# One PSUM bank for a sort opened earlier, and a block's transposes halved, in a graph-network kernel

## The chip, the core and the metric

The kernel runs on one core of a Trainium2 chip. A core has five engines, each with its own in-order list of instructions: TensorE (PE in the profile; its weight loads are PEld), VectorE (DVE), ScalarE (ACT), GpSimd (POOL) and SyncE (SP). They work side by side and wait for one another through semaphores. SP, ACT and POOL also issue DMAs. Matmuls write into PSUM, which has eight banks of 2 KB per partition; the other working memory is SBUF. The metric is the device time of one execution in microseconds.

## The reference

The input is a batch of 16 graphs: `x` (16, 1024, 64), a symmetric 0/1 adjacency `adj` (16, 1024, 1024) with a unit diagonal, and a node mask. Four graph layers follow one another, each in the form

```python
h = jnp.maximum(_layernorm(x, axis=-1), 0.0)
x = x + layer(h, adj, ...)
```

Layer 0 thins out the neighbours of nodes with many of them, and then takes, for each node and channel, three quantiles (0.25, 0.5, 0.75) over the values of the remaining neighbours, weights them by 0.25, 0.5, 0.25 into `agg`, and applies a two-layer perceptron to `h + agg`. Its core is

```python
vals = jnp.where(nd[..., None], x[:, None, :, :], jnp.inf)
s = jnp.sort(vals, axis=2)
v_lo = jnp.take_along_axis(s, idx_lo, axis=2)[:, :, 0, :]
v_hi = jnp.take_along_axis(s, idx_hi, axis=2)[:, :, 0, :]
agg = agg + w * (v_lo + frac * (v_hi - v_lo))
```

Layer 1 is a gated recurrent update of a message `A @ m`. Layer 2 is a message `adjacency @ h` and a small perceptron. Layer 3 is an attention over the adjacency with a softmax and `attention @ h`.

## The kernel before

The 16 graphs are worked on as 8 pairs (numbered 0 to 7 here). For a pair, these pieces of work exist:

- **The sort** (`sort_begin`, `sort_pair`). The 64 channels of two graphs fill 128 partitions, and a bitonic network of 55 steps sorts 1024 nodes in each. `sort_begin` loads x (L700), normalizes it (lines L662 to L672, with a Sqrt on ACT in L666), writes h_d and p_d, and transposes h on PE into a PSUM tile `ps` (L714), which ACT copies out (L717). A step of the network is three DVE operations: which pairs swap (L729), the larger (L736), the smaller (L737). Four steps' masks go to DRAM in one DMA (m_d, L740). Then the network is run backwards on the ranks with the masks read again (`swapped`, L749; DVE lines L753, L754, L760): the way back. At the end the ranks are transposed on PE into `ps` (L799), copied by ACT (L800) and written (y_d, L802). Tables of value differences go to t_d and w_d.
- **Neighbours** (`neighbours`, called by `prepare`). The adjacency is loaded in 512 KB blocks (`a`, L819, two buffers), thinned out with scans on DVE (L820, L825), squares on ACT (L854 to L856) and block matmuls on PE (L875), and a transposed copy is written to DRAM (a_d, L834).
- **The selection** (`weights`, `select`), once for each graph of the pair. Counting matmuls (L1045) and their evictions find each node's place in the sorted list; transposes (L1101) and sign evictions (L1103) make step functions of them; matmuls with tables of differences (L1148) and predicated copies (L1156) give the values. A compact step (from L1207) gathers up to 64 nodes of each graph that fall outside the windows of the first pass.
- **The extra block** (`extras`), once for a pair. The gathered rows are loaded (`comb_x`, L1257). In each of three rounds, ACT shifts them into `y_x` (L1275, two buffers), PE transposes 16 chunks of 128 x 112 into the PSUM tile `tr` (L1282), ACT makes two sign tiles of it (L1285), and DVE takes maxima of `y_x` in place (L1289, L954, L950, L1295, L1296). Some 25 small DVE operations (`places`) follow. Then six sums: PE fills `cand` (L1306, one buffer of four banks), DVE picks (L1011) and adds (L1018, L1020). Last, a selection matrix `sel_t` (one buffer, loaded on SP, L1314) puts the results back: a matmul into `tr` (L1317) and a predicated copy (L1318), once per graph.
- **The layers** (`layers`), for the pair's two graphs with separate pools: the perceptron and layers 1 to 3. The adjacency's transposed blocks are loaded three times (adjT, L1402) and multiplied (L1409). The last operations of a graph's DVE work are L1516 and L1519 of the attention.

The loop over pairs writes: selection of pair `pr`, the extra block, the layers, then neighbours and sort of pair `pr + 1`, and then `sort_begin` of pair `pr + 2`. The order on the engines is not the written order. A scheduler at build time takes the instructions by priority, as soon as by its own estimate their inputs and buffers are ready, and lays them down as one fixed list per engine. So sort steps and neighbours of a later pair stand among the instructions of the selection and the layers. Buffers of one name rotate in the written order: the sort's rows, `code` and masks of pair `pr + 2` follow those of `pr + 1`, and `sort_begin` of `pr + 2` needs the tile `ps` after `sort_pair` of `pr + 1`.

PSUM sets one limit. In the second half of the loop's body, `nbp` (neighbours) has two banks. During the extra block, `xp` has `tr` (two banks) and `cand` (four): all eight are taken. During the layers, `lb0` has three banks, `lb1` two and the sort's pool `sop` one: eight again. `sop` is opened when `xp` is closed, so the sort's two transposes, the one that ends a sort (L799) and the one that begins the next (L714), come after the extra block.

Of the kernel before, what the change touches and what calls it, by code (L numbers as in the profile page):

```python
# [9 lines left out]
F32 = mybir.dt.float32  # L10
BF16 = mybir.dt.bfloat16
# [3 lines left out]
I16 = mybir.dt.int16  # L15
F16 = mybir.dt.float16
F8 = mybir.dt.float8e5
AF = mybir.ActivationFunctionType
ALU = mybir.AluOpType
AX = mybir.AxisListType  # L20
PSUM = bass.MemoryType.PSUM
DRAM = bass.MemoryType.DRAM

P = 128
# [11 lines left out]
NH = NW // 2  # L36
# [6 lines left out]
def gnn_stack(ctx, tc, x, adj, nodemask, w, out):  # L43
# [10 lines left out]
    nc = tc.nc  # L54
    B, N, C = x.shape
# [9 lines left out]
    ident_b = const.tile([P, P], BF16, name="ident_b")  # L65
# [876 lines left out]
    NQ = C // 4  # L942
    SHR, SHL, AND, XOR = ALU.logical_shift_right, ALU.logical_shift_left, ALU.bitwise_and, ALU.bitwise_xor

    def maxima(yu, n):

        while n > 1:
            if n % 2 and n > 3:
                n -= 1
                nc.vector.tensor_tensor(  # L950
                    yu[:, :, :, :4], yu[:, :, :, :4], yu[:, :, :, n * 4 : n * 4 + 4], op=ALU.max
                )
            h = n // 2
            nc.vector.tensor_tensor(  # L954
                yu[:, :, :, : h * 4], yu[:, :, :, : h * 4], yu[:, :, :, (n - h) * 4 : n * 4], op=ALU.max
            )
            n -= h
# [66 lines left out]
    before = (half, lower)  # L1024
# [226 lines left out]
    def extras(pr, kept, aggs, xs, xp):  # L1251

        vx = kept["vx"]
        comb = xs.tile([P, NW * C], F32, name="comb_x")
        for u in range(0, len(PIECES), 2):
            at = slice(PIECES[u] * 512, (PIECES[u] + len(PIECES[u : u + 2])) * 512)
            nc.scalar.dma_start(comb[:, at], x_d[:, at])  # L1257
        tabs = []
        for i in range(2):
            tab = xs.tile([4 * NH, NQ, 4, 48], F16, name=f"tab{i}")  # L1260
            nc.vector.memset(tab, 0.0)
            for d in range(4):
                taken = nc.sync.dma_start(
                    tab[d : 4 * NH : 4, :, d, :],
                    t_d[(pr * 2 + i) * C : (pr * 2 + i + 1) * C, :NH].rearrange("(q d) h e -> d h q e", d=4)[d],
                )
            tabs.append(tab)
        qx = xs.tile([P, 3], F32, name="qx")
        nc.vector.tensor_scalar(qx, vx[:, :3], -2048.0, -2048.0, op0=ALU.mult, op1=ALU.add)
        signs = []  # L1270
        z = xs.tile([P, 1, 6, C], U16, name="z_x")
        odd = xs.tile([P, 1, 6, C], U16, name="odd_x")
        for k in range(3):
            y = xs.tile([P, 2, 2 * NQ, 4 * NH], I16, name="y_x", bufs=2)
            nc.scalar.activation(  # L1275
                y[:, 0].rearrange("p r (h d) -> p r h d", d=4),
                comb.rearrange("p (h r d) -> p r h d", r=2 * NQ, d=4),
                AF.Identity, bias=qx[:, k : k + 1], scale=1.0,
            )
            pt = xp.tile([P, 2, 512], F32, name="tr").bitcast(BF16).rearrange("p e (q n) -> p (e q) n", n=P)  # L1280
            for q in range(NQ):
                nc.tensor.transpose(pt[: 4 * NH, q, :], y[:, 0, q, :].bitcast(BF16), ident_b)  # L1282
            for s in range(2):
                sign = xs.tile([4 * NH, NQ, P], F16, name="sign_x", bufs=6)
                nc.scalar.activation(  # L1285
                    sign, pt[: 4 * NH].bitcast(I16), AF.Sign, bias=before[s][: 4 * NH], scale=-1.0
                )
                signs.append(sign)
            nc.vector.tensor_scalar_add(y[:, 1], y[:, 0], 2048.0)  # L1289
            yu = y.bitcast(U16)  # L1290
            maxima(yu, NH)
            ev, od = yu[:, :, :NQ, :4], yu[:, :, NQ:, :4]
            zs = z[:, 0, 2 * k : 2 * k + 2, :].rearrange("p s (q d) -> p s q d", d=4)
            os_ = odd[:, 0, 2 * k : 2 * k + 2, :].rearrange("p s (q d) -> p s q d", d=4)
            nc.vector.tensor_tensor(zs, ev, od, op=ALU.max)  # L1295
            nc.vector.tensor_tensor(os_, od, ev, op=ALU.is_gt)  # L1296
        marks = places(xs, z, 6 * C, 1)
        aggx = xs.tile([P, C], F32, name="agg_x")
        ag = aggx.rearrange("p (q d) -> p q d", d=4)
        for s in range(6):  # L1300
            cand = xp.tile([P, NQ, P], F32, name="cand")
            for q in range(NQ):
                for part in range(2):
                    for i in range(2):
                        mine = slice(i * ROOM, (i + 1) * ROOM)
                        nc.tensor.matmul(  # L1306
                            cand[mine, q, :96], signs[s][:, q, mine], tabs[i][:, q, :, part * 24 : (part + 1) * 24],
                            start=(part == 0), stop=(part == 1),
                        )
            v = pick(cand[:, :, :96], [mk[:, 0, s, :] for mk in (odd, *marks)])  # L1310
            add_to(ag, s == 0, v, vx[:, 3 + s : 4 + s])
        for i in range(2):
            sel_t = xs.tile([P, NT, P], F32, name="sel_t")
            nc.sync.dma_start(sel_t, sel_d[i])  # L1314
            ps = xp.tile([P, 2, 512], F32, name="tr")[:, 0, :].rearrange("p (t c) -> p t c", c=C)
            for t in range(NT):
                nc.tensor.matmul(ps[:, t, :], sel_t[:, t, :], aggx, start=True, stop=True)  # L1317
            nc.vector.copy_predicated(  # L1318
                aggs[i], kept["flag"][i].rearrange("p (t o) -> p t o", o=1).to_broadcast([P, NT, C]), ps
            )  # L1320
        return taken.ins if hasattr(taken, "ins") else taken
# [230 lines left out]
    def side_pools():  # L1552
        return (
            tc.tile_pool(reuse_waits="tile", name="nb", bufs=1),
            tc.tile_pool(reuse_waits="tile", name="nbp", bufs=2, space=PSUM),
        )

    pairs = B // 2
    nb_, nbp_ = side_pools()
# [7 lines left out]
    for pr in range(pairs):  # L1567
        with tc.tile_pool(reuse_waits="tile", name="keep", bufs=1) as keep:
            aggs = [keep.tile([P, NT, C], F32, name=f"agg{i}") for i in range(2)]
            kept = {  # L1570
                "flag": [keep.tile([P, NT], U16, name=f"flag{i}") for i in range(2)],
                "vx": keep.tile([P, 9], F32, name="vx"),
            }
            with tc.tile_pool(reuse_waits="tile", name="kn", bufs=1) as kn:
                with (
                    tc.tile_pool(reuse_waits="tile", name="sy", bufs=2) as sy,
                    tc.tile_pool(reuse_waits="tile", name="sw", bufs=1) as sw,
                    tc.tile_pool(reuse_waits="tile", name="sg", bufs=2) as sg,
                    tc.tile_pool(reuse_waits="tile", name="sp", bufs=2, space=PSUM) as sp,
                    tc.tile_pool(reuse_waits="tile", name="sc", bufs=2, space=PSUM) as sc,  # L1580
                ):
                    for i in range(2):
                        wt, positive = weights(pr * 2 + i, kn, None if i else taken)
                        select(pr * 2 + i, i, wt, positive, *made[i], aggs[i], kept, sw, sg, sy, sc, sp)
            nb_, nbp_ = side_pools()
            with nb_ as nb, nbp_ as nbp:
                with tc.tile_pool(reuse_waits="tile", name="xs", bufs=1) as xs, tc.tile_pool(reuse_waits="tile", name="xp", bufs=1, space=PSUM) as xp:
                    taken = extras(pr, kept, aggs, xs, xp)
                with (
                    tc.tile_pool(reuse_waits="tile", name="ly0", bufs=1) as ly0,  # L1590
                    tc.tile_pool(reuse_waits="tile", name="ly1", bufs=1) as ly1,
                    tc.tile_pool(reuse_waits="tile", name="lb0", bufs=3, space=PSUM) as lb0,
                    tc.tile_pool(reuse_waits="tile", name="lb1", bufs=2, space=PSUM) as lb1,
                    tc.tile_pool(reuse_waits="tile", name="sop", bufs=1, space=PSUM) as sop,
                ):
                    for i, (ly, lb) in enumerate(((ly0, lb0), (ly1, lb1))):
                        layers(pr * 2 + i, (pr * 2 + i) % 4, aggs[i], ly, lb)
                    if pr + 1 < pairs:
                        made = prepare(pr + 1, nb, nbp)
                        sort_pair(pr + 1, cur, sop)  # L1600
                    if pr + 2 < pairs:
                        cur = sort_begin(pr + 2, sop)
# [47 lines left out]
```

## Time and profile before

| | us |
|---|---|
| median of 3 runs | 6483.81 |
| lowest and highest run | 6482.19, 6496.31 |
| span of the profiled execution | 6475.2 |
| DVE busy | 5339.2 (82%) |
| PE busy | 4545.8 (70%) |
| ACT busy | 3530.8 (55%) |
| one pair in the middle of the run, from attention's end to attention's end | 775 |

The profile is of one execution. Its busy times per engine are sums over the whole span; the slices cut the span in 40 equal parts and give the busy share in tenths. A row of busy times by stage gives the stretch's start and end, its length, and then for each engine the busy time and the number of instructions in it, the granted TensorE clock, the DMA share and the GB/s. A row of a group of instructions gives the line, engine, operation, tiles and shapes, the count, then busy time and mean ns of one, and last the idle time of that engine just before them with what ended it. The span is 6.99 us under the lowest run's time and 8.61 us under the median.

### The profile page before, as it was taken

What the parts mean: (1) busy time and instruction counts of PE and PEld (TensorE: products, weight loads), DVE (VectorE), ACT (ScalarE), POOL (GpSimd) and SP (SyncE); (2) the same over time, 40 slices, a digit from 0 to 9 for tenths busy, and PEclk for the clock granted to TensorE, in tenths of its full rate; (3) what the DMA queues carried; (4) which work ended last, traced back from release to release, by engine and by line L of the source; (5) the groups of instructions that cost most, each with busy time, mean ns of one, the idle gap of its engine ahead of it and who ended that gap; (6) DMA issues with size and microseconds to landing.
All of it is one profiled execution on the core that took longest, in us unless ns stands there. A gap on an engine that the chain in (4) does not pass through costs nothing.

```text
span 6475.2 us, 112886 instructions
## 1 busy us (share of the span) xinstructions
PE 4545.8 (70%) x45010; PEld 2849.6 (44%) x45010; DVE 5339.2 (82%) x13031; ACT 3530.8 (55%) x4337; POOL 138.4 (2%) x234
## 2 busy tenths in 40 slices
PE   3177766776777858678577776777766776778856
PEld 2144542544435544355433554345543544435542
DVE  7999979997699976999679986899869997576655
ACT  4165555655556555556555565565565655555623
POOL 1000000000000000000000000000000000000000
PEclk7588868888788978888788886888868887788967
DMA  4311254112531126211361104511154112520014
GB/s 121 98 38 47 73 157 146 44 54 71 170 114 46 46 74 205 71 54 34 99 207 55 55 23 135 188 49 50 53 150 148 42 52 67 174 75 16 7 57 140
DMA packets 525639, 568.14 MB, mean 88 GB/s; under 512 B 265004, under 2 KB 414894, under 8 KB 525102
## 3 DMA queue, kind: packets, MB, share of 16 engines
q1 hardware_dynamic: 381472, 476.43, 24.1%
q10 hardware_dynamic: 142862, 82.31, 4.1%
q8 instruction: 355, 5.82, 0.4%
q0 software_dynamic: 768, 2.10, 0.1%
q14 instruction: 182, 1.49, 0.1%
HBM read 376.95 MB, written 183.76 MB: 87 GB/s over the span
## 4 chain that ended last, share of the span: by engine, by line
PE 36%; DVE 33%; ACT 13%; DMA 10%; issue 7%; SPq 1%; POOL 0%; ACTq 0%; DVEq 0%; POOLq 0%
PE comb L1045 13%; PE cand L1148 6%; ACT sign L1103 5%; DMA adjT<-a_d 4%; DVE y L1119 4%; PE comb L1101 3%; PE bank L1409 3%; PE comb L1236 2%; DVE att L1519 2%; DVE cand L1156 2%; DVE cum L825 2%; DMA a<-in_adj_dram 2%; DVE code L760 2%; DVE adjT L1513 2%; ACT y L1055 2%
## 5 line engine op out<-in xcount | busy, mean ns | idle before, releaser
L1045 PE MATMUL comb<-wt,ndT 128*128 128x512 fp8e5 x6144 | 1503.0, 401 | 26.1 <-DVE top L1516 11.1
L1055 ACT ACTIVATE y<-comb,qb 128x1024 int16<-128x1024 f32 (+1 forms) x640 | 632.0, 1026 | 954.0 <-PE comb L1045 953.5
L1045 PEld LDWEIGHTS <-ndT 128*128 128x128 fp8e5 x6144 | 615.3, 103 | 794.4 <-issue 188.5
L1119 DVE TENSOR_TENSOR y<-y 128x512 uint16<-128x512 uint16 (+5 forms) x896 | 705.3, 790 | 92.6 <-PE comb L1101 60.0
L1148 PE MATMUL cand<-vtab,sign 128*128 128x48 f16 (+1 forms) x18432 | 701.9, 194 | 105.1 <-DVE agg L1018 53.7
L1148 PEld LDWEIGHTS <-sign 128*128 128x128 fp8e5 x18432 | 668.0, 98 | 174.9 <-issue 76.8
L1101 PE MATMUL comb<-ident_b,y 128*128 128x128 bf16 x4608 | 392.2, 254 | 413.1 <-ACT sign L1103 363.1
L1103 ACT ACTIVATE sign<-comb,half 128x2048 fp8e5<-128x2048 int16 (+1 forms) x384 | 591.9, 1541 | 140.0 <-PE comb L1101 130.7
L1156 DVE COPY_PREDICATED cand<-w_f,cand 128x256 f32<-128x256 uint16 (+1 forms) x1536 | 535.2, 378 | 137.4 <-PE cand L1148 134.0
L1103 ACT ACTIVATE sign<-comb,lower 128x2048 fp8e5<-128x2048 int16 (+1 forms) x384 | 591.3, 1540 | 0.0
L1101 PEld LDWEIGHTS <-y 128*128 128x128 bf16 x4608 | 357.4, 115 | 437.1 <-issue 430.5
L1409 PE MATMUL bank<-adjT,nd 128*64 128x512 f32 x1024 | 304.4, 657 | 66.4 <-DMA adjT<-a_d 65.5
L1409 PE MATMUL bank<-att,hs 128*64 128x512 f32 x512 | 195.6, 871 | 202.7 <-ACT hs L1524 200.9
L729 DVE TENSOR_TENSOR swapped<-s 128x512 uint16<-128x512 f32 x440 | 301.5, 685 | 41.6 <-ACT s L717 36.6
L825 DVE TENSOR_TENSOR_SCAN cum<-ni 128x1024 f16<-128x1024 fp8e5 x128 | 292.9, 2290 | 41.9 <-ACT sq L854 23.6
L875 PE MATMUL pk<-minus_b,rem 128*128 128x128 bf16 x1024 | 222.4, 245 | 132.2 <-ACT rem L856 132.2
L875 PE MATMUL pk<-ident_b,ni 128*128 128x128 bf16 x1024 | 219.4, 241 | 129.3 <-ACT ndT L881 68.4
L833 ACT COPY at<-pk 128x512 f32<-128x512 f32 x256 | 146.7, 587 | 289.5 <-PE pk L831 139.2
L736 DVE TENSOR_TENSOR s<-s 128x512 f32<-128x512 f32 (+2 forms) x440 | 288.9, 657 | 0.0
L921 DVE TENSOR_SCALAR wt<-node 128x2048 uint8<-128x2048 f16 x224 | 269.3, 1217 | 23.6 <-PE comb L1236 23.5
L737 DVE TENSOR_TENSOR s<-s 128x512 f32<-128x512 f32 (+2 forms) x440 | 288.7, 656 | 0.0
L760 DVE TENSOR_TENSOR code<-code,xo 128x1024 uint16<-128x1024 uint16 x360 | 264.8, 736 | 5.2
(301 smaller groups left out, 8100.0 us busy)
## 6 DMA issues: line engine op xcount, KB each, us to landing
adjT<-a_d SPq DMA_DIRECT2D x384, 512.0 KB
a<-in_adj_dram SPq DMA_DIRECT2D x128, 512.0 KB
a_d<-at ACTq DMA_DIRECT2D x256, 256.0 KB
m_d<-swapped SPq DMA_DIRECT2D x104, 512.0 KB
swapped<-m_d SPq DMA_DIRECT2D x104, 512.0 KB
n_d<-nat SPq DMA_DIRECT2D x128, 128.0 KB
x_d<-xr SPq DMA_DIRECT2D x48, 256.0 KB
comb_x<-x_d ACTq DMA_DIRECT2D x24, 512.0 KB
```

The costliest lines, as they stand in the source:

```text
L729: nc.vector.tensor_tensor(side(swapped[:, k, :], j), hi, lo, op=ALU.is_gt)
L760: nc.vector.tensor_tensor(pairs_, pairs_, d2, op=ALU.bitwise_xor)
L825: nc.vector.tensor_tensor_scan(cum[:, t - t0, :], ni[:, t, :], wide[:, t, pad - 1 : pad - 1 + N], 0.0, op0=ALU.add, op1=ALU.add)
L875: nc.tensor.matmul(pk[:, n % 4, :], lhs, rhs, start=(n % 4 == 0 and m == 0), stop=(m == len(terms) - 1 and last),)
L1045: nc.tensor.matmul(pw[:, e, :], ndT[:, j, t * P : (t + 1) * P], piece[:, j].rearrange("p w c -> p (w c)"), start=(j == 0), stop=(j == NT - 1),
L1055: nc.scalar.activation(y[:, 0, chunks, at : at + words_ * d_].rearrange("p q (w d) -> p q w d", d=d_), by_word[:, : words_ * C].rearrange( ...
L1101: nc.tensor.transpose(pt[:, q - q0, :], y[:, 0, q, :].bitcast(BF16), ident_b)
L1103: nc.scalar.activation(signs[tl][s][:, q0:q1, :], pt.bitcast(I16), AF.Sign, bias=before[s], scale=-1.0, saturate=False,)
L1119: nc.vector.tensor_tensor(v[:, :, :, :n], v[:, :, :, :n], v[:, :, :, n : 2 * n], op=ALU.max)
L1148: nc.tensor.matmul(cand[:, e, at : at + 12 * d_].rearrange("p (d l) -> p d l", l=12), signs[tl][sec][:, chunk, :], tab[:, q, :, half_ * 12 ...
L1156: nc.vector.copy_predicated(v[:, :, :, dst : dst + k], mk.to_broadcast([P, 2, C // 2, k]), v[:, :, :, frm : frm + k])
L1409: nc.tensor.matmul(po[to : to + C, :], lhs, rhs[:, f * HALF : (f + 1) * HALF], start=(j == 0), stop=(j == NT - 1))
```

## The change

The pool `sop`, one PSUM bank, is now opened before the extra block and stays open over it and the layers. To make room, the extra block's tile `tr` has one bank instead of two. The 16 transposes of a round are made in two halves of eight through that one bank, and each half is evicted by its own two sign instructions, of 1024 columns instead of 2048; the two sign tiles of a round are allocated before the halves. The matmul that puts the results back used one of the two banks of `tr` and now uses its only one.

```diff
@@ -1277,15 +1277,17 @@
                 comb.rearrange("p (h r d) -> p r h d", r=2 * NQ, d=4),
                 AF.Identity, bias=qx[:, k : k + 1], scale=1.0,
             )
-            pt = xp.tile([P, 2, 512], F32, name="tr").bitcast(BF16).rearrange("p e (q n) -> p (e q) n", n=P)
-            for q in range(NQ):
-                nc.tensor.transpose(pt[: 4 * NH, q, :], y[:, 0, q, :].bitcast(BF16), ident_b)
-            for s in range(2):
-                sign = xs.tile([4 * NH, NQ, P], F16, name="sign_x", bufs=6)
-                nc.scalar.activation(
-                    sign, pt[: 4 * NH].bitcast(I16), AF.Sign, bias=before[s][: 4 * NH], scale=-1.0
-                )
-                signs.append(sign)
+            both_signs = [xs.tile([4 * NH, NQ, P], F16, name="sign_x", bufs=6) for s in range(2)]
+            for q0 in range(0, NQ, NQ // 2):
+                pt = xp.tile([P, 512], F32, name="tr").bitcast(BF16).rearrange("p (q n) -> p q n", n=P)
+                for q in range(NQ // 2):
+                    nc.tensor.transpose(pt[: 4 * NH, q, :], y[:, 0, q0 + q, :].bitcast(BF16), ident_b)
+                for s in range(2):
+                    nc.scalar.activation(
+                        both_signs[s][:, q0 : q0 + NQ // 2, :], pt[: 4 * NH].bitcast(I16), AF.Sign,
+                        bias=before[s][: 4 * NH], scale=-1.0,
+                    )
+            signs += both_signs
             nc.vector.tensor_scalar_add(y[:, 1], y[:, 0], 2048.0)
             yu = y.bitcast(U16)
             maxima(yu, NH)
@@ -1312,7 +1314,7 @@
         for i in range(2):
             sel_t = xs.tile([P, NT, P], F32, name="sel_t")
             nc.sync.dma_start(sel_t, sel_d[i])
-            ps = xp.tile([P, 2, 512], F32, name="tr")[:, 0, :].rearrange("p (t c) -> p t c", c=C)
+            ps = xp.tile([P, 512], F32, name="tr").rearrange("p (t c) -> p t c", c=C)
             for t in range(NT):
                 nc.tensor.matmul(ps[:, t, :], sel_t[:, t, :], aggx, start=True, stop=True)
             nc.vector.copy_predicated(
@@ -1583,7 +1585,7 @@
                         wt, positive = weights(pr * 2 + i, kn, None if i else taken)
                         select(pr * 2 + i, i, wt, positive, *made[i], aggs[i], kept, sw, sg, sy, sc, sp)
             nb_, nbp_ = side_pools()
-            with nb_ as nb, nbp_ as nbp:
+            with nb_ as nb, nbp_ as nbp, tc.tile_pool(reuse_waits="tile", name="sop", bufs=1, space=PSUM) as sop:
                 with tc.tile_pool(reuse_waits="tile", name="xs", bufs=1) as xs, tc.tile_pool(reuse_waits="tile", name="xp", bufs=1, space=PSUM) as xp:
                     taken = extras(pr, kept, aggs, xs, xp)
                 with (
@@ -1591,7 +1593,6 @@
                     tc.tile_pool(reuse_waits="tile", name="ly1", bufs=1) as ly1,
                     tc.tile_pool(reuse_waits="tile", name="lb0", bufs=3, space=PSUM) as lb0,
                     tc.tile_pool(reuse_waits="tile", name="lb1", bufs=2, space=PSUM) as lb1,
-                    tc.tile_pool(reuse_waits="tile", name="sop", bufs=1, space=PSUM) as sop,
                 ):
                     for i, (ly, lb) in enumerate(((ly0, lb0), (ly1, lb1))):
                         layers(pr * 2 + i, (pr * 2 + i) % 4, aggs[i], ly, lb)
```

Lines below the first hunk stand two lines later in the changed kernel, and lines below the loop's pools one line later.

## The prediction

> **What bounds the kernel now.** I read the page's busy shares and slices first, then the busy time by stage, then the vector engine's order of time inside one stage.
>
> ```profile
> PE 4545.8 (70%) x45010; PEld 2849.6 (44%) x45010; DVE 5339.2 (82%) x13031; ACT 3530.8 (55%) x4337; POOL 138.4 (2%) x234
> DVE  7999979997699976999679986899869997576655
> ```
>
> VectorE (DVE) is the busiest engine, and its low digits recur once per pair. So I cut a pair at four marks on DVE: the end of the pair before (its last L1519), the first L1207, the last L1156, the last L1318, its own last L1519. I call the stages select-1, select-2, extra and layers. First pair 4, then pair 7, which carries no sort and prepares no later pair:
>
> ```profile
> core 0: us, PE busy (x) PEld busy (x) DVE busy (x) ACT busy (x) POOL busy (x), PEclk, DMA share, GB/s
> 3454.90:3646.00 191.10, 146.94 (x1684) 97.37 (x1682) 187.16 (x457) 126.04 (x151) 0.00 (x0) 0.86 0.14 49
> 3646.00:3917.70 271.70, 211.31 (x2378) 140.20 (x2379) 231.93 (x605) 141.67 (x167) 3.69 (x7) 0.85 0.18 50
> 3917.70:4012.50 94.80, 48.26 (x714) 41.94 (x714) 60.13 (x126) 61.89 (x65) 2.73 (x9) 0.62 0.41 107
> 4012.50:4230.20 217.70, 158.46 (x861) 75.92 (x859) 184.15 (x441) 111.46 (x163) 9.39 (x12) 0.82 0.55 174
> ...
> 5761.90:5943.60 181.70, 146.15 (x1712) 96.94 (x1710) 121.43 (x313) 123.07 (x143) 0.00 (x0) 0.89 0.03 9
> 5943.60:6200.90 257.30, 201.59 (x2346) 131.38 (x2346) 165.43 (x456) 136.94 (x159) 2.03 (x2) 0.88 0.10 26
> 6200.90:6278.80 77.90, 29.98 (x464) 27.99 (x464) 44.19 (x96) 21.10 (x9) 0.32 (x2) 0.52 0.15 39
> 6278.80:6462.80 184.00, 121.98 (x397) 47.91 (x399) 99.39 (x266) 59.77 (x88) 2.90 (x4) 0.74 0.42 136
> ```
>
> To be seen: the selects hardly care how much sort DVE carries. Pair 7 has 132 us less DVE work there and is only 24 us shorter; something else, mostly TensorE (PE) and its evictions, holds them at 182 + 257. The extra stage is different: a chain of small steps with 34.7 us of DVE waits. What ends them:
>
> ```profile
> L954 DVE TENSOR_TENSOR y_x<-y_x 128x256 uint16<-128x256 uint16 (+3 forms) x15 | 12.8, 852 | 3.6 <-PE tr L1282 3.2
> L1011 DVE COPY_PREDICATED cand<-odd_x,cand 128x768 f32<-128x768 uint16 x6 | 5.8, 961 | 9.6 <-PE cand L1306 9.6
> L820 DVE TENSOR_SCALAR ni<-a 128x1024 fp8e5<-128x1024 f32 x6 | 4.1, 684 | 5.4 <-DMA a<-in_adj_dram 5.4
> L1289 DVE TENSOR_SCALAR y_x<-y_x 128x3584 int16<-128x3584 int16 x3 | 3.3, 1088 | 5.6 <-ACT y_x L1275 5.6
> L1318 DVE COPY_PREDICATED agg<-flag,tr 128x512 f32<-128x512 uint16 x2 | 1.5, 728 | 8.2 <-PE tr L1317 8.2
> ```
>
> The profiled span is 6475.2 us, 8.6 under the runs' median of 6483.8; I sum on the span and add 8.6.
>
> **What the bank moves.** I compared the instruction order of the two built programs, engine by engine, and gave each DVE operation the mean time from its start to the next start in the profile (forward sort steps L729, L736, L737: 0.60 us, as in the order of time at 199.63, 200.23, 200.95). DVE's total stays 5337 us; only places change. In pairs 2 to 5, us before and after:
> - select-1 190 to 185: 90 forward operations leave (-54), 105 of the way back (L753 to L760, 0.47 each) come (+50).
> - select-2 232 to 182: those 105 leave.
> - extra 59 to 105: 43 forward operations (27), the next norm (35 operations, 6) and 18 of neighbours (12) come.
> - layers 184 to 193: 47 forward operations come (+28), 18 of neighbours and the norm leave (-18).
>
> Select-2: pair 7's and pair 4's rows give (271.7-257.3)/(231.9-165.4) = 0.22 us of span per us of DVE, so -11; ends 0 and -14 (pair 7's 257). Select-1 was 98% busy: between -0.7 (slope 0.14) and -5; I take -3. Its way back reads the masks that SP loads (L749); bufs=2 gives four steps, 5.6 us, of cover.
>
> Layers: the slope between pair 6 (202.9 us for 137.2 busy) and pair 4 is 0.31, so +9 for 28 us of steps; less 2 for the norm and 6 for neighbours (0.5 per us, pair 6 to pair 7). Here the adjacency loads no longer queue behind the h_d writes on SP, but the first nd loads now stand behind two more `a` loads. Taken +2, ends -5 and +10.
>
> Extra: with no wait left it lasts its 104.6 us of DVE work, +10; with all 34.7 us of waits left, 139, +45. I follow the order. Covered: the cand waits (9.6: three to six steps now stand between one add and the next pick), `a` (5.4) and nearly all of the L1317 wait (8.2: 2.4 and 6.1 us of neighbours). Not covered: the first L1289 (5.1: as little as before stands ahead) and the tr waits (3.2). But the steps also stand between dependent picks, where there was no wait to fill: that is why the sum, not the old chain, rules. 104.6 + 5.1 + 3.2 + 1 for the rest = 114.
>
> **Queues passed.** SP gets x loads, y_d, h_d, p_d, the code load and three m_d writes inside this stage; in the layers two y_d took 3.2 us to issue, two p_d 3.2, two h_d 1.3, so some 10 us. Before, SP waited from 3947.9 to 3973.6 for an `a` buffer; that covers it, and if it did not, L820 would wait again by up to 5.4. The second sel_t load now stands behind three m_d writes, the third of which needs 36 forward operations done; by then they are, 6 us before its use. ACT gets L706, two L717 and a Sqrt with its table load (1.28 + 0.30) ahead of the third round's signs. POOL (2% busy) only takes its ni and mask steps in another order, at no cost while it idles.
>
> **The two halves.** A 2048-wide sign took 1.95 us, 1.85 from start to start. A 1024-wide one from this bank is not in the trace: between half, 0.93, and the 1024-wide L855's 1.18; I take 1.05, nearest to both. Six more per pair cost ACT 6 x 0.12 = 1 us. The larger cost is the wait: with one bank, the second eight transposes start after both signs of the first eight (2.1 us), and L954, which overwrites y_x in place, waits for the last transpose. Three rounds: 6.3, plus 1.6 for the Sqrt, less 3.3 of norm that stands under the first: +4.6. Ends: 0, hidden under DVE's other work, and 8.
>
> The Trainium skill's "Perfetto Trace Analysis", section Optimizing Tensor Performance, says that matmul groups should rotate through PSUM banks so that evictions overlap the next group; this speaks against one bank for two halves. The row that agrees is TensorE's 5.1 us wait for the signs before L1282 now; by the rule alone all of the 6.3 us would show, 50 us over eight pairs. "ScalarE: Activation LUTs" (What ACT_TABLE_LOAD costs) gives 280 + 0.833 ns per element, less 93 of overlap, so 1.04 us from start to start at 1024; no run here shows it yet.
>
> **Sum.** Extra 114 + 4.6 = 119, +24. Pairs 2 to 5: -3 - 11 + 24 + 2 = +12 each, 48. Pair 1 (select-1 unchanged, select-2 28 us lighter): -6 + 24 + 2 = +20. Pair 0 (selects unchanged; extra 85 to 92, layers 171 to 193): +9 + 6 = +15. Pair 6 (no sort follows it): -3 - 11 + 9 - 1 = -6. Pair 7: halves, +6. Total +83: span 6558, time 6567.
>
> **Rivals.**
> *The bank does its work: faster.* The steps fill waits only, and the halves hide: extra 105 (+10), select-2 -14, select-1 -5, layers 0: -9 in each of pairs 2 to 5, +4 in pair 1 (-6 + 10), -13 in pair 6 (-5 - 14 + 6), +7 in pair 0: -38, 6446 in all; with layers at -5 in five pairs, 6421. For it: DVE waits 112 us of a pair's 775. Against: 40 of them are in select-2, where taking 50 us of work out only adds waits. It decides where extra ends below 107 us.
> *Steps in the way everywhere.* All old waits stay (extra 139) as SP's and ACT's longer queues take the place of the covered ones: 20 more in five pairs, 6667. For it: ACT's queue is in order and its signs, Sqrt and L717 stand in the chain. Against: cand and L1317 waits are ended by PE, whose order is little changed.
> *The start moves but nothing else matters*: only the halves show, 8 x 6 = +48, 6532. The moved orders speak against it.
>
> **How the numbers follow.** Forecast with the halves-only case, 6497 to 6620: 0.51. Queues and waits, above 6620: 0.24. Faster: 0.17. In between: 0.08. Under 0.2%, 13 us, a measurement here can't tell from no change. Five pairs' extra at its ends gives -71 and +103, selects and layers together about 45 and 73 either way; by squares -84 and +126 about 6567. That is 6483 to 6693; I take 6465 to 6680, to hold part of the faster case without more than 2 in 10 left out.
>
> **What would show it.** In the changed profile: the m_d writes begin inside the extra stage; extra near 119 with DVE over 85% busy; the cand wait gone and a longer one before L954; select-2 near 261; pair 7's extra 6 longer. It is wrong if extra stays under 107, or if select-1, now holding nearly the whole way back, stalls on its mask loads.

## The result and the profile after

The changed kernel takes 6576.5 us (median of 4 runs, 6573.64 to 6581.87); the kernel before, run beside it, takes 6486.39 us. The ratio is 1.0143, with a 95% interval of 1.0128 to 1.0157: the change costs about 90 us. The profiled execution of the changed kernel has a span of 6580.0 us, 104.8 more than the one before.

The page's busy times and DVE's slices of the changed kernel:

```profile
PE 4589.4 (70%) x45010; PEld 2862.8 (44%) x45010; DVE 5355.1 (81%) x13031; ACT 3532.6 (54%) x4385; POOL 156.1 (2%) x234
DVE  7999979996899778996789877898689976576645
```

DVE's work has hardly changed (5339.2 to 5355.1 us), so the 105 us are waits or work in a worse place. The slices are somewhat more even, with more sevens and eights among the nines and sixes, since DVE is busier in the extra blocks and less busy in the selections. Busy time by stage, pair 4's four stages and then pair 7's extra block, in the changed kernel (start and end, length, then busy time and number of instructions of each engine):

```profile
core 0: us, PE busy (x) PEld busy (x) DVE busy (x) ACT busy (x) POOL busy (x), PEclk, DMA share, GB/s
3520.30:3708.60 188.30, 145.31 (x1684) 95.39 (x1682) 182.65 (x469) 124.70 (x151) 0.00 (x0) 0.88 0.17 53
3708.60:3976.80 268.20, 209.62 (x2380) 136.62 (x2380) 187.35 (x502) 142.50 (x167) 3.68 (x7) 0.87 0.13 33
3976.80:4096.90 120.10, 64.55 (x808) 56.08 (x808) 102.02 (x224) 71.19 (x85) 9.82 (x13) 0.60 0.49 134
4096.90:4312.80 215.90, 151.51 (x757) 69.89 (x756) 192.41 (x430) 102.35 (x147) 6.12 (x8) 0.79 0.52 166
6294.30:6377.10 82.80, 30.85 (x464) 28.47 (x464) 44.50 (x96) 22.23 (x15) 0.32 (x2) 0.50 0.14 37
```

The reader is to see where DVE's work went and what each stage made of it. Select-2 lost 45 us of DVE work and became 3.5 us shorter. The extra block got 42 us of DVE work and became 25 us longer; DVE is now busy in 85% of it. Both are pair 4's; the means stand below. Pair 7, which carries no sort and no neighbours, is 5 us longer in its extra block: that is the halves alone. Means of pairs 2 to 5, from the same marks:

| us | before | after | difference |
|---|---|---|---|
| select-1 | 190.6 | 188.9 | -1.7 |
| select-2 | 272.6 | 269.1 | -3.5 |
| extra | 94.5 | 118.2 | +23.7 |
| layers | 217.2 | 215.8 | -1.4 |
| whole pair | 775.0 | 792.0 | +17.0 |

What DVE did in pair 4's extra block, in groups of instructions by line (count, then busy us and mean ns, then idle time just before, with what ended it). Lines behind the transposes are two higher than before:

```profile
L954 DVE TENSOR_TENSOR y_x<-y_x 128x256 uint16<-128x256 uint16 (+3 forms) x15 | 12.8, 853 | 4.6 <-PE tr L1284 4.2
L729 DVE TENSOR_TENSOR swapped<-s 128x512 uint16<-128x512 f32 x15 | 10.5, 700 | 0.1
L737 DVE TENSOR_TENSOR s<-s 128x512 f32<-128x512 f32 x14 | 9.6, 683 | 0.0
L736 DVE TENSOR_TENSOR s<-s 128x512 f32<-128x512 f32 x14 | 9.5, 681 | 0.0
L820 DVE TENSOR_SCALAR ni<-a 128x1024 fp8e5<-128x1024 f32 x10 | 6.9, 686 | 2.5 <-DMA a<-in_adj_dram 2.2
L1011 DVE COPY_PREDICATED cand<-odd_x,cand 128x768 f32<-128x768 uint16 x6 | 5.8, 958 | 2.3 <-PE cand L1308 2.2
L1291 DVE TENSOR_SCALAR y_x<-y_x 128x3584 int16<-128x3584 int16 x3 | 3.3, 1088 | 4.1 <-ACT y_x L1275 4.1
L1320 DVE COPY_PREDICATED agg<-flag,tr 128x512 f32<-128x512 uint16 x2 | 1.5, 726 | 1.1 <-PE tr L1319 1.1
```

The 43 operations of forward sort steps are there (L729, L736, L737; three make a step), and work did come into the waits: that for `cand` fell from 9.6 to 2.2 us, that for the put-back from 8.2 to 1.1, that for `a` from 5.4 to 2.2. DVE's order of time shows why this was no gain. The fourth of the six sums in pair 4 (start, length):

```profile
4059.86 0.96 DVE L1011 COPY_PREDICATED cand<-odd_x,cand 128x768 f32<-128x768 uint16 x1
4060.73 0.69 DVE L736 TENSOR_TENSOR s<-s 128x512 f32<-128x512 f32 x1
4061.33 0.42 DVE L1011 COPY_PREDICATED cand<-w_f,cand 128x256 f32<-128x256 uint16 x1
4061.66 0.69 DVE L737 TENSOR_TENSOR s<-s 128x512 f32<-128x512 f32 x1
4062.26 0.42 DVE L1011 COPY_PREDICATED cand<-w_f,cand 128x256 f32<-128x256 uint16 x1
4062.59 0.69 DVE L729 TENSOR_TENSOR swapped<-s 128x512 uint16<-128x512 f32 x1
4063.20 0.29 DVE L1011 COPY_PREDICATED cand<-w_f,cand 128x128 f32<-128x128 uint16 x1
4063.39 0.69 DVE L736 TENSOR_TENSOR s<-s 128x512 f32<-128x512 f32 x1
4064.00 0.22 DVE L1011 COPY_PREDICATED cand<-w_e,cand 128x64 f32<-128x64 uint16 x1
```

The picks (L1011) depend on one another, and between any two of them stands one of the sort's operations. PE can refill `cand` only after the last pick, so each operation there lengthens the chain by itself, 0.6 us each time, besides those that fill the wait after the sum. Of the 43, 21 stand between the first pick of a sum and its add, 12.9 us in all. From first pick to add, the second to sixth sums of pair 4 take 19.0 us together before and 30.5 after.

Select-2, on the other side, has waits in place of the work that left. What DVE waited for in pair 4's select-2, before and then after (total us, number of times, longest):

```profile
DVE cand L1156 <- PE cand L1148: 14.1, 4, 11.3
DVE y L1114 <- ACT y L1055: 6.0, 1, 6.0
```

```profile
DVE y L1114 <- ACT y L1055: 30.1, 4, 11.9
DVE cand L1156 <- PE cand L1148: 15.9, 8, 11.4
DVE y L1119 <- PE comb L1101: 8.6, 6, 4.5
DVE y L1119 <- ACT sign L1103: 7.6, 2, 3.8
```

### The profile page after: what moved, and what is told of

Read it like the earlier page. It is cut to its first block, busy times and chain, and to the rows that moved or that the text cites. A ratio compares the mean times of both kernels' runs of the same rounds, so it can differ in the third digit from the quotient of the medians.

```text
span 6580.0 us, 112906 instructions
## 1 busy us (share of the span) xinstructions
PE 4589.4 (70%) x45010; PEld 2862.8 (44%) x45010; DVE 5355.1 (81%) x13031; ACT 3532.6 (54%) x4385; POOL 156.1 (2%) x234
## 4 chain that ended last, share of the span: by engine, by line
PE 42%; DVE 24%; ACT 18%; DMA 10%; issue 4%; SPq 1%; POOL 0%; ACTq 0%; DVEq 0%
PE comb L1045 15%; PE cand L1148 7%; ACT sign L1103 5%; PE comb L1101 4%; PE bank L1411 4%; DMA adjT<-a_d 3%; DVE y L1119 3%; PE comb L1236 2%; ACT y L1055 2%; DMA a<-in_adj_dram 2%; DVE att L1521 2%; DVE adjT L1515 2%; PE pk L875 2%; DMA a_d<-at 1%; DVE cum L825 1%
## 5 line engine op out<-in xcount | busy, mean ns | idle before, releaser
L1114 DVE TENSOR_SCALAR y<-y 128x4608 int16<-128x4608 int16 x128 | 173.4, 1354 | 224.0 <-ACT y L1055 223.8
L825 DVE TENSOR_TENSOR_SCAN cum<-ni 128x1024 f16<-128x1024 fp8e5 x128 | 294.3, 2303 | 32.0 <-ACT sq L854 20.6
L729 DVE TENSOR_TENSOR swapped<-s 128x512 uint16<-128x512 f32 x440 | 302.9, 688 | 6.6
L736 DVE TENSOR_TENSOR s<-s 128x512 f32<-128x512 f32 (+2 forms) x440 | 290.5, 660 | 0.0
L737 DVE TENSOR_TENSOR s<-s 128x512 f32<-128x512 f32 (+2 forms) x440 | 289.8, 659 | 0.0
```

The lines of the kernel that those rows point to most:

```text
L729: nc.vector.tensor_tensor(side(swapped[:, k, :], j), hi, lo, op=ALU.is_gt)
L736: nc.vector.tensor_tensor(to_lo, lo, hi, op=ALU.max)
L825: nc.vector.tensor_tensor_scan(cum[:, t - t0, :], ni[:, t, :], wide[:, t, pad - 1 : pad - 1 + N], 0.0, op0=ALU.add, op1=ALU.add)
```

## The experiments

The theory after the result: sort steps in the extra block, above all those between its dependent picks, cost about 20 us in each of the five pairs that have them, and the halves through one bank about 5 us in each pair. The rival was that the single bank, by its waits, is the larger part. All stage times below are means over pairs 2 to 5, taken between the prediction's marks.

**1. The halves alone.** The pool `sop` is opened with the layers' pools again, as before; `tr` keeps one bank and two halves.

```diff
-            with nb_ as nb, nbp_ as nbp, tc.tile_pool(reuse_waits="tile", name="sop", bufs=1, space=PSUM) as sop:
+            with nb_ as nb, nbp_ as nbp:
...
                     tc.tile_pool(reuse_waits="tile", name="lb1", bufs=2, space=PSUM) as lb1,
+                    tc.tile_pool(reuse_waits="tile", name="sop", bufs=1, space=PSUM) as sop,
```

> Only the halves through one bank; the sort's pool is opened after the extra block, as before. In the built order the sort still moves: 45 forward steps and the norm stand in the extra stage of pairs 1 to 5 (DVE work 104 us there), because the extra block's pool then leaves one of eight banks free. Theory (the steps that stand in the extra chain cost, whatever let them in): extra 116 to 120 us in pairs 2 to 5, pair 7's 83, time 6565 to 6590, as the whole change. Rival (the pool's earlier opening is what costs): extra near 100, pair 7's 83, time 6520 to 6535.

6560.49 us, ratio 1.0114 (1.0094 to 1.0135); extra 116.1, pair 7's extra 82.9. The time is just under what the theory gave and far above the rival. The reason is in the order on DVE: 45 operations of forward steps and the norm stand in the extra block although the pool is opened behind it. Neighbours' two banks, `cand`'s four and `tr`'s one leave the eighth bank free, and the scheduler, which goes by its own estimate of when a bank is free, begins the sort there; experiment 2, where no bank is free, has none of it there. So of the change's two parts, the narrower `tr` alone lets the sort in; where the pool is written matters little.

**2. Halves, with two one-bank buffers.** Experiment 1's kernel, with two buffers for `tr`. All eight banks are taken again, so the sort can't begin, and the halves take turns.

```diff
-                pt = xp.tile([P, 512], F32, name="tr").bitcast(BF16).rearrange("p (q n) -> p q n", n=P)
+                pt = xp.tile([P, 512], F32, name="tr", bufs=2).bitcast(BF16).rearrange("p (q n) -> p q n", n=P)
...
-            ps = xp.tile([P, 512], F32, name="tr").rearrange("p (t c) -> p t c", c=C)
+            ps = xp.tile([P, 512], F32, name="tr", bufs=2).rearrange("p (t c) -> p t c", c=C)
```

> The halves alone, through two banks in turn (two buffers of one bank); the sort's order is as before, 59 us of DVE work in the extra stage. Theory (the halves cost by the wait for the one bank, 5 us a pair): extra 95 to 97, pair 7's 78 to 79, time 6483 to 6500. Rival (the split of six signs into twelve costs by itself, in instructions and in places between them): extra 99 to 101, pair 7's 83, time 6515 to 6530.

6446.29 us, ratio 0.9953 (0.9936 to 0.997): faster than before, which neither theory had. Extra is 86.7, 8 us under before, while pair 7's is 77.6, no shorter than before's 77.9. In pair 7 nothing else runs on DVE beside the extra block, and the halves show there as they are. ACT's order of time at that place, the changed kernel first, then this one (start, length, idle time before it and what ended it):

```profile
6305.36 1.11 ACT L1286 ACTIVATE sign_x<-tr,lower 112x1024 f16<-112x1024 int16 x1
6308.05 1.11 ACT L1286 ACTIVATE sign_x<-tr,half 112x1024 f16<-112x1024 int16 x1 [1.58 <-PE tr L1284]
6309.06 1.11 ACT L1286 ACTIVATE sign_x<-tr,lower 112x1024 f16<-112x1024 int16 x1
6311.62 1.11 ACT L1286 ACTIVATE sign_x<-tr,half 112x1024 f16<-112x1024 int16 x1 [1.45 <-PE tr L1284]
```

```profile
6168.91 1.11 ACT L1286 ACTIVATE sign_x<-tr,lower 112x1024 f16<-112x1024 int16 x1
6169.90 1.11 ACT L1286 ACTIVATE sign_x<-tr,half 112x1024 f16<-112x1024 int16 x1
6170.90 1.12 ACT L1286 ACTIVATE sign_x<-tr,lower 112x1024 f16<-112x1024 int16 x1
6171.90 1.13 ACT L1286 ACTIVATE sign_x<-tr,half 112x1024 f16<-112x1024 int16 x1
```

With one bank, ACT waits about 1.5 us at each new half for PE, which itself had to wait for the signs; with two it doesn't. The difference is 82.9 against 77.6, 5.3 us a pair. This is what the Trainium skill's "Perfetto Trace Analysis" (Optimizing Tensor Performance) advises, to rotate matmul groups through banks, and here the runs agree. A sign of 1024 columns goes from start to start in 1.00 us (6169.90 to 6170.90); "ScalarE: Activation LUTs" (What ACT_TABLE_LOAD costs) gave the prediction an estimate of 1.04.

But where the 8 us in the other pairs come from was open: from the banks, or from another order of the neighbours' work. Experiments 5 to 10 are on that.

**3. The sort held back.** The changed kernel, with `sort_begin` ordered behind the extra block's last copy (`put`, the predicated copy into `agg`).

```diff
-                        cur = sort_begin(pr + 2, sop)
+                        with tc.issue_after(put):
+                            cur = sort_begin(pr + 2, sop)
```

> The whole change, but sort_begin's DVE operations are issued after the extra block's last one. In the built order no forward step and no norm is left in the extra stage (DVE work 65 us instead of 105), select-2 has 220 us instead of 182. Theory (the steps in the extra chain are the main cost): extra 102 to 106 in pairs 2 to 5 instead of 118, time 6500 to 6535. Rival (the longer SP and ACT queues and the one bank cost it, DVE's steps only fill waits): extra 114 to 120, time 6560 to 6590.

6488.61 us, ratio 1.0007 (0.9997 to 1.0016); extra 98.1, pair 7's extra still 82.8. Nearly all of the change's cost is gone, the bank and the halves being as in the changed kernel. That is more than the theory gave; extra was 4 us below its lower end. Pair 4's extra block here:

```profile
3926.20:4024.70 98.50, 52.06 (x776) 44.47 (x775) 66.43 (x134) 64.63 (x74) 3.76 (x11) 0.65 0.39 109
```

Of the sort nothing is left in it, neither steps nor norm. The 6 us of DVE work above before's 60.3 are neighbours: 37 of their operations stand in the block, against 30 before and 44 in the changed kernel. So the hold takes out more than the steps: the norm, and 7 of the neighbours' operations (6 us) that came in with the sort. Two readings speak for the steps as the larger part. The second to sixth sums of pair 4 fall from 30.5 us to 19.9, nearly to before's 19.0, and between their picks and adds the neighbours' work in all six sums goes only from 12.0 to 9.7 us, the sort's from 12.9 to none. And pair 6, which has no sort to begin, has the same 7 more of neighbours' operations in the changed kernel as here, and its extra block is 5.0 us longer than before (97.1 against 92.1), no more than pair 7's, which has none of them: these operations cost nothing that shows beside the halves. How the 20 us divide between the steps, the norm and the neighbours that came with them is not shown. The other stages nearly cancel: the layers are 6 us shorter than in the changed kernel (209.7), and select-2 is 6 us longer (275.4).

**4. Whole rounds, the sort free.** The 16 transposes go whole through two of the four banks of a `cand` tile, with 2048-wide signs as before; `sop` is opened early.

```diff
-            both_signs = [xs.tile([4 * NH, NQ, P], F16, name="sign_x", bufs=6) for s in range(2)]
-            for q0 in range(0, NQ, NQ // 2):
-                pt = xp.tile([P, 512], F32, name="tr").bitcast(BF16).rearrange("p (q n) -> p q n", n=P)
...
+            pt = xp.tile([P, NQ, P], F32, name="cand").rearrange("p q n -> p (q n)")[:, : NQ * P // 2]
+            pt = pt.bitcast(BF16).rearrange("p (q n) -> p q n", n=P)
+            for q in range(NQ):
+                nc.tensor.transpose(pt[: 4 * NH, q, :], y[:, 0, q, :].bitcast(BF16), ident_b)
```

> The bank is open early and the sort's steps stand in the extra stage (DVE work 106 us there in pairs 1 to 5), but the 16 transposes of a round stay whole: they go through two of cand's four banks, and signs stay 2048 wide. Theory: extra is the sum of DVE work and the waits that nothing fills, 112 to 117 in pairs 2 to 5; pair 7's extra 78; time 6525 to 6550, the whole change less 5 us a pair. Rival (the halves in one bank carry the loss): extra 95 to 101, time 6475 to 6500.

6521.29 us, ratio 1.0068 (1.0051 to 1.0084); extra 114.7, pair 7's extra 78.6. Extra is where the theory had it: without any halves, 101 us of DVE work still make it 115. The median is a little under the theory's range; the layers are 207.6 instead of 215.8.

**5. Rounds in turn.** As 4, but the three rounds use the tile's banks 0-1, 2-3 and 0-1.

```diff
-            pt = xp.tile([P, NQ, P], F32, name="cand").rearrange("p q n -> p (q n)")[:, : NQ * P // 2]
-            pt = pt.bitcast(BF16).rearrange("p (q n) -> p q n", n=P)
+            if k == 0:
+                rounds = xp.tile([P, NQ, P], F32, name="cand").rearrange("p (e q) n -> p e (q n)", e=2)
+            pt = rounds[:, k % 2, :].bitcast(BF16).rearrange("p (q n) -> p q n", n=P)
```

> The kernel of the fourth experiment (16 transposes whole, through two of cand's banks, sort free from the start of the extra block), except that the three rounds take banks 0-1, 2-3 and 0-1 of one cand tile in turn, so that the second round's transposes need not wait for the first round's signs. The order on DVE is as in the fourth (106 us of work in the extra block). Theory (the 8 us that two half-size banks took off the extra block came from rounds that no longer wait for one another's signs): extra 105 to 109 instead of 114.7, layers 207 to 210, median 6455 to 6490. Rival (the 8 us came from the place of the neighbours' work, not from the banks): extra 113 to 116, median 6510 to 6530.

6523.87 us, ratio 1.0081 (1.0064 to 1.0098); extra 114.6, as in 4. The theory falls: rounds that needn't wait for each other's signs bring nothing.

**6. Rounds in turn, the sort held.** As 5, with `sort_begin` behind the extra block as in 3.

> The same, with sort_begin of the pair after next held behind the extra block's last copy, as in the third experiment: 59 us of DVE work in the extra block, as before. Theory (sort steps in the extra block cost 20 us a pair, banks in turn save 8): extra 85 to 91, layers 207 to 214, median 6420 to 6455, level with or a little below two half-size banks. Rival (the bank for the sort costs by itself, or the turn of banks brings nothing): extra 94 to 99, median 6475 to 6495.

6468.9 us, ratio 0.9994 (0.9984 to 1.0003); extra 96.5, so the rival is right, and the bank for the sort, opened early but not used there, brings neither gain nor loss. (The kernel before took 6473.16 us beside experiments 5 to 8, 13 less than beside the others, so the ratio says more than the median here.) Pair 4's extra block, in 5 and then here:

```profile
3938.70:4053.50 114.80, 58.40 (x808) 50.59 (x806) 101.23 (x226) 70.18 (x79) 8.91 (x13) 0.66 0.50 143
3928.90:4025.60 96.70, 50.89 (x694) 44.98 (x694) 60.16 (x126) 61.79 (x64) 2.52 (x8) 0.59 0.41 113
```

Against 5, the sort's beginning and some 15 of the neighbours' operations, which leave with it, cost 18 us in the extra block and 55 us of the median; select-2, 5.7 us a pair shorter in 5, gives some of it back. Between the changed kernel and 3 it was 20 us and 88. The two rows also answer a rival that no expectation named, the granted TensorE clock. Over the whole span it was 0.811 before and 0.797 in the changed kernel, but the shorter extra block here has the lower clock (0.59 against 0.66), so the clock doesn't make the difference in this stage.

**7. Neighbours later.** The kernel before, with no bank touched; the second half of the first graph's neighbours is ordered behind the extra block's last copy.

```diff
+            order = ExitStack()
+            if t0 and behind is not None:
+                order.enter_context(tc.issue_after(behind))
             for t in range(t0, t0 + HT):
...
-                        made = prepare(pr + 1, nb, nbp)
+                        made = prepare(pr + 1, nb, nbp, put)
```

> The kernel before, with the second half of the first graph's neighbours of the next pair held behind the extra block's last copy; no bank is touched. DVE work in the extra block falls from 59 to 47 us, in the layers from 184 to 170; select-1 gets 20 more, select-2 5 more. Theory (other work between dependent picks costs its own length, whatever work it is): extra 83 to 88 instead of 94.5, with the waits for an adjacency block gone, layers 207 to 215, select-1 and select-2 together 3 to 5 longer, median 6420 to 6465. Rival (only sort steps are in the way, neighbours fill waits): extra 92 to 96 with DVE waits grown from 35 to 45 or more, median 6480 to 6510.

6582.13 us, ratio 1.0171 (1.0154 to 1.0188). The part on the extra block came as the theory said: 12 us less DVE work there, and 83.6 instead of 94.5 us, with as much waiting in it as before (34 us in pair 4). The sum did not, for the work had to go somewhere. The stages of pair 4 in this kernel:

```profile
core 0: us, PE busy (x) PEld busy (x) DVE busy (x) ACT busy (x) POOL busy (x), PEclk, DMA share, GB/s
3488.70:3702.30 213.60, 160.80 (x1856) 103.56 (x1855) 207.93 (x485) 133.24 (x163) 0.00 (x0) 0.87 0.13 47
3702.30:3977.20 274.90, 212.12 (x2379) 139.76 (x2380) 236.72 (x619) 143.15 (x167) 3.95 (x7) 0.87 0.18 51
3977.20:4059.70 82.50, 36.95 (x535) 32.54 (x534) 48.13 (x108) 39.32 (x33) 0.93 (x4) 0.56 0.33 92
```

Select-1, 98% busy before, got 21 us of DVE work and became 23 us longer. The expectation had 3 to 5, together with select-2. In this stage, which DVE filled already, work cost its length.

**8. Neighbours later, two one-bank buffers.** Experiments 2 and 7 together.

> Halves through two one-bank buffers (second experiment) and the neighbours' late half together. Theory (the 8 us of the second experiment came from the banks): the two add up, extra 77 to 81, near the 77.6 of pair 7, which has no neighbours; median 6385 to 6425. Rival (the 8 us came from where the neighbours' steps and their wait for an adjacency block fell): nothing adds, extra as long as in the late half alone or at most 2 us shorter, median within 15 of it.

6581.95 us, ratio 1.0157 (1.0137 to 1.0176); extra 82.3, 1.3 us under 7. The rival is right: with the neighbours placed alike, the two banks bring next to nothing in these pairs, so the 8 us of experiment 2 came mostly from where the neighbours' work fell; experiments 9 and 10 move that work by itself.

**9. Only the scans later.** The kernel before; only the scans (L825) of the first graph's second half are ordered behind the first of the six adds.

```diff
-                nc.vector.tensor_tensor_scan(
+                with tc.issue_after(behind) if t0 and behind is not None else ExitStack():
+                    nc.vector.tensor_tensor_scan(
...
-            add_to(ag, s == 0, v, vx[:, 3 + s : 4 + s])
+            added = add_to(ag, s == 0, v, vx[:, 3 + s : 4 + s])
+            sum0 = added if s == 0 else sum0
...
-                        made = prepare(pr + 1, nb, nbp)
+                        made = prepare(pr + 1, nb, nbp, sum0)
```

> The kernel before, banks and transposes untouched, with only the scans (L825) of the first neighbours' second half held behind the first of the extra block's six adds (L1018). In the order on DVE two scans, 4.5 us, leave the place ahead of that add and come after it, as they stand in the kernel of the second experiment. Theory (that kernel's gain came from where the neighbours' scans stand, not from its banks): extra 85 to 89 instead of 94.5, median 6435 to 6460. Rival (it came from the two banks and the shorter signs): extra 92 to 95, median 6470 to 6490.

6404.47 us, ratio 0.9874 (0.986 to 0.9889): the fastest of all, and it changes no bank. DVE's order around the first add in pair 4, before and then in this kernel (lines one higher):

```profile
3963.22 2.28 DVE L825 TENSOR_TENSOR_SCAN cum<-ni 128x1024 f16<-128x1024 fp8e5 x1
3965.42 0.21 DVE L1011 COPY_PREDICATED cand<-w_e,cand 128x64 f32<-128x64 uint16 x1
3965.54 2.28 DVE L825 TENSOR_TENSOR_SCAN cum<-ni 128x1024 f16<-128x1024 fp8e5 x1
3967.73 0.26 DVE L1018 TENSOR_SCALAR agg_x<-cand,vx 128x64 f32<-128x64 f32 x1
3970.86 0.96 DVE L1011 COPY_PREDICATED cand<-odd_x,cand 128x768 f32<-128x768 uint16 x1 [2.86 <-PE cand L1306]
```

```profile
3936.50 0.23 DVE L1012 COPY_PREDICATED cand<-w_e,cand 128x64 f32<-128x64 uint16 x1
3936.77 0.28 DVE L1019 TENSOR_SCALAR agg_x<-cand,vx 128x64 f32<-128x64 f32 x1
3936.97 4.46 DVE L826 TENSOR_TENSOR_SCAN cum<-ni 128x1024 f16<-128x1024 fp8e5 x2
3941.35 0.94 DVE L1012 COPY_PREDICATED cand<-odd_x,cand 128x768 f32<-128x768 uint16 x1
```

Two scans stood ahead of the add, 4.4 us in the chain, and then DVE waited 2.86 us for PE's next group. Behind the add they run while PE fills `cand`, and the wait is gone. Extra is 89.5, 5 us shorter than before though half a microsecond above the theory's range, and it decides against the rival. The stage table shows more:

```profile
3424.80:3615.00 190.20, 149.15 (x1715) 96.32 (x1713) 183.47 (x439) 124.74 (x147) 0.00 (x0) 0.89 0.13 43
3615.00:3891.40 276.40, 211.55 (x2378) 139.65 (x2379) 243.42 (x638) 144.14 (x173) 3.94 (x7) 0.86 0.20 56
3891.40:3982.40 91.00, 47.02 (x676) 40.91 (x674) 60.61 (x125) 60.53 (x62) 2.58 (x8) 0.64 0.41 111
3982.40:4185.90 203.50, 153.25 (x864) 71.93 (x861) 173.00 (x424) 111.17 (x163) 10.61 (x13) 0.84 0.59 183
```

Some 10 us of DVE work moved from the layers to select-2 in the scheduler's new order. Means: select-2 +4, layers -12 (205.4), extra -5. The larger part of the gain is in the layers, and no expectation had it; why the layers gain 12 us for 10 us less work is not shown.

**10. The scans later, two one-bank buffers.** Experiments 2 and 9 together.

> The same hold on the scans, and the halves through two one-bank buffers of the second experiment. The order of the six sums on DVE is nearly that of the second experiment. Theory (banks bring nothing, order does): within 2 us of extra, and 10 us of the median, of the run beside it that has the hold alone. Rival (banks bring the 8 us): extra 6 to 9 below that run, median 30 to 50 below it.

6437.02 us, ratio 0.9922 (0.9908 to 0.9936). Extra is 87.5, 2.0 below 9, on the theory's edge; a gain of 8 by the banks is excluded. The median is 33 us above 9, which neither had: the layers are 212.9 there instead of 205.4. So two banks are worth up to 2 us in an extra block that carries neighbours, and the layers, which have 6 us more DVE work than in 9, more than take that back.

## Why the prediction was right, and where not

The prediction was 6567 (6465 to 6680), slower at 0.75; it is 6576.5. By its own steps:

- **Extra 114 + 4.6 = 119, +24: right.** 118.2, +23.7. Its rule, that DVE's work rules and not the old chain, held: 102 us of work and some 16 to 18 us of waits, where 104.6 and 13.9 had been put. These two misses, 3 us each, cancel, so that the sum comes out within 1 us is luck. The waits it called covered are mostly covered, and the first L1291 wait it left uncovered took 4.1 (taken 5.1). Experiments 3 and 6 show the cause: with the sort's beginning held back, the stage falls to 98.1 and 96.5.
- **The halves, +4.6 (ends 0 and 8), pair 7 +6: right.** Pair 7's extra block is 5.0 longer, and with two buffers it isn't. By the rule of rotating banks alone the prediction had 6.3 a pair; the 5.0 to 5.3 lie between. Its two smaller terms, 1.6 for the Sqrt and 3.3 for the norm, no run shows by themselves. (Its 1 us more for ACT is 1.5 by its own figures, 12 x 1.05 less 6 x 1.85, and 0.9 by the measured 1.00; it stands in no sum.) Where sort steps run beside them, the halves cost less than in pair 7: experiment 4, with no halves, is only 3.5 us shorter in the extra block than the changed kernel.
- **Select-2, -11 (ends 0 and -14): wrong in size.** -3.5. The slope of 0.22 us per us of DVE work came from pair 7 against pair 4, but pair 7 differs in more than DVE: its rows also have 10 us less PE work (201.59 against 211.31). From experiment 4 (186.2 us of DVE work, 267.7 long) to 9 (243.4, 276.5), the slope is 0.15; from before to after it is 0.08. The wait rows above show the rest: in pair 4, 45 us of work left, and 41 us of waits came.
- **Select-1, -3: near.** -1.7, and the mask loads made DVE wait for 1.5 us once in pair 4. But the slope of 0.14 behind its smaller bound fits neither way: 3.5 us less work made the stage 1.7 us shorter here, and experiment 7 put work in at 1.08 us per us.
- **Layers, +2 (ends -5 and +10): within its ends, not explained.** -1.4 in the mean.
- **The sum.** The eight pairs give +16, +16, four of +17 in the mean, -4 and +8, which is +104 in the profiled execution, against +15, +20, four of +12, -6 and +6, so +83. Select-2 alone accounts for 6 to 11 us in each of the pairs 2 to 6, and the layers give some of it back. Between the medians the change costs 90 us, so the sum is 7 us short; between the profiled executions it costs 104.8, and the sum is 21 us short. Before's profiled execution (6475.2) is shorter than every run timed beside the changed kernel (6482.19 and up), and the changed kernel's is the slowest of its four, so the second overstates the miss.
- **The bank does its work: faster.** It would have needed an extra block below 107; with the steps in it, none of the runs had one under 114. With the steps held back (98.1 and 96.5) the kernel is level with the one before and still not faster: select-2, with 221 us of DVE work instead of 232.6, lasts 275.4 us in experiment 3, no shorter than before.
- **The start moves but nothing else matters.** Its 5 to 6 us per pair for the halves exist, but experiment 1 shows a thing that no case had: the narrower `tr` brings the moved order with it, with or without the moved pool.
- **Steps in the way everywhere (6667)** fell: SP issued the `m_d` writes inside the extra block, as predicted, yet the waits for `a` (5.4 to 2.2) and at the put-back (8.2 to 1.1) became shorter.

What stays open: why the layers take 215.8 us in the changed kernel, 210 in experiments 1, 3, 5 and 6, 205.4 in 9 and 217 in 7. DVE's busy time there (193, 186, 191, 189, 192, 173, 169) doesn't order them. Nor does the granted clock: in pair 4's layers it was 0.82 before (217.7 us), 0.79 in the changed kernel (215.9) and 0.79 in experiment 4 (208.3). The waits differ in name from kernel to kernel, and no run isolates one.

## What to carry to other kernels

A wait on the busiest engine isn't room for other work unless that work can stand inside the wait. Between picks that depend on one another, every foreign operation added its own length here, and this scheduler, which goes by priority, put 21 of the sort's 43 operations there. Before freeing a PSUM bank, ask which work that bank was holding back, because the tightness may be what keeps the order good. And find out which stage is full: a microsecond of DVE work was worth 0.08 to 0.15 us in select-2 and 1.08 in select-1.

## What the runs showed that was not expected

- A bank that is free is enough for the scheduler to start the next sort; where its pool is opened in the program decided little (experiment 1 against the changed kernel: 6560.49 against 6576.5 us, 45 against 43 operations of forward steps in the extra block).
- Ordering one half's scans behind one add of 0.28 us, which moved two of them, took 82 us off the kernel, more than every change of banks (6404.47 against 6486.23 us). About 5 us a pair are the scans' place; some 12 us a pair are a change in the order of the layers that followed from it.
- Rotating whole rounds through PSUM (114.6 against 114.7 us) brought nothing, while rotating halves brought 5.3 us in pair 7: it paid only where the eviction would otherwise have stopped the next transposes within one round.
